# A graph network with routed experts: the second product of the first layer's experts by seven block products

## The chip, the cores and the metric

The kernel runs on one core of one Trainium2 chip. A core has a matrix engine (TensorE, PE in the profile, with its weight loads shown as PEld), a vector engine (VectorE, DVE), an engine for activation functions (ScalarE, ACT), a general one (GpSimd, POOL) and one that mostly starts transfers (SyncE, SP). Each works through its own list of instructions in order, and waits for the others through semaphores. Data lie in HBM, in the core's memory of 128 partitions (SBUF), or in the banks into which TensorE sums (PSUM). The metric is the device time of one execution in microseconds (us); the figure used is the median of several runs.

## The reference

There are 3327 nodes with 256 features, and an adjacency matrix of 3327 by 3327 with few entries. Two layers follow each other:

```
x = x + relu(adj @ (layernorm(x) @ W) + b)                       # layer 0, graph
x = x + experts_0(layernorm(x))                                  # 8 experts, hidden width 1024, relu
x = x + relu(f(adj) @ (tanh(layernorm(x) @ Wp + bp) @ Wg) + bg)  # layer 1, f: tanh(adj^2), the top 700 of a row
x = x + experts_1(layernorm(x))                                  # 8 experts, hidden width 256, gelu, added to its input
```

The experts of layer 0 are what the change is about. Each token's scores for the eight experts are `x Wg^T + bg`; the two best are taken, and a softmax of the two gives their weights:

```
for e in range(8):
    h = relu(x @ W1[e].T + b1[e])
    y = h @ W2[e].T + b2[e]
    out = out + combine[:, e] * y      # combine is zero but for a token's two experts
```

The kernel computes an expert only for the tokens that chose it. All is in float32.

## The kernel before, in words

**Tokens and blocks.** The nodes are padded to 26 tiles of 128. While the graph part of layer 0 is at work, VectorE computes the routing scores of finished tiles (L659, one instruction for each tile and expert, reading the tile `gate`, which holds one layer's eight gate vectors on every partition). GpSimd then scatters each token's normalized row, with its weight and its place, into a list in HBM that is ordered by expert (`xlist`, L779). Experts work on blocks of 256 rows of that list, all of one expert. The blocks are numbered by steps `t`. There are 30 steps in the arm of the program that runs: 26 blocks of 256 rows (two row groups of 128) and four of 128 rows (one row group; "singles", at t = 12, 17, 22 and 27).

**One step.** `step` (L1231) does the following.

- It starts the loads of block `t + 2` (L1101 to L1150: the tokens' rows, the two weight matrices of 1 MB each, and the biases), on SyncE's queue, into the ring places that block `t - 1` left.
- `first` (L1164) computes the hidden layer, transposed: for each of eight pieces of 128 hidden units, two matmuls of width 256 (L1171) into one of two PSUM buffers (`psh`), and one ScalarE instruction that adds the bias and takes the relu (L1178).
- `turned` (L1152) turns the next block's tokens: four transposes on TensorE (L1157) into the same kind of buffer, and a copy to SBUF (L1161). The function that copies is a parameter of `experts`: VectorE's `tensor_copy` for layer 0, ScalarE's `copy` for layer 1.
- `second` (L1181) computes the output: for each of the two row groups, eight matmuls of width 256 that sum into one bank (L1209). VectorE adds the bias (L1216) and multiplies by the row's weight (L1217), and GpSimd scatters the 128 rows to the token's places in HBM (`ys`, L779).

**Order.** The program text is not yet the order on the engines. A planner orders each engine's instructions by its own estimates and by the data dependences. `tc.issue_after`, mostly through the helper `behind`, forces some instructions behind a named one: in the experts the indices of the scatter (L1187 to L1192) stay behind the last scaling of the block before (`last_y`), and other work for VectorE is put behind the same mark.

**Around the experts.** The first steps, t = 0 to 2, overlap the end of the graph part; the last tokens are routed during step 0, and a plan for the late blocks is made on VectorE during steps 2 and 3. During the last steps VectorE adds the outputs that are ready (`add_begun`, L1462) and computes statistics of the next normalization (L1616). After the last step, `between` (L1510) loads the other outputs from `ys` (L1280), adds them to `x` (L1293), normalizes, and computes the features for the graph part of layer 1. The gate vectors of layer 1 are loaded into the same tile `gate` by a transfer of 1 MB on GpSimd's queue (L1419), after the last score of layer 0 and step 1; the trace has its issue at 335.6 us.

Of the kernel before, what the change touches and what calls it, by code (L numbers as in the profile page):

```python
# [10 lines left out]
F32 = mybir.dt.float32  # L11
BF16 = mybir.dt.bfloat16
I32 = mybir.dt.int32
AF = mybir.ActivationFunctionType
ALU = mybir.AluOpType
# [7 lines left out]
P = 128  # L23
NT = 26
NP = NT * P
D = 256
DC = D // P
# [18 lines left out]
SG = SB // P  # L46
# [4 lines left out]
WT, ID = D, D + 1  # L51
# [61 lines left out]
def places_of(loads, ends, free):  # L113

    at = {}
    for i, q in enumerate(loads):
        at[q] = free[i] if i < RING else at[ends[i - RING]]
    return at, [at[q] for q in ends[len(loads) - RING :]]
# [3 lines left out]
AT0, BLOCKS0 = places_of(LOADS[0], ENDS[0], list(range(RING)))  # L122
# [5 lines left out]
def gnn_moe_two_layers(  # L128
# [24 lines left out]
    nc = tc.nc  # L153
# [3 lines left out]
    work = ctx.enter_context(tc.tile_pool(name="work", bufs=3))  # L157
    dram = ctx.enter_context(tc.tile_pool(name="dram", bufs=1, space=bass.MemoryType.DRAM))
    psh = ctx.enter_context(tc.tile_pool(name="psh", bufs=2, space=PSUM))
    psy = ctx.enter_context(tc.tile_pool(name="psy", bufs=4, space=PSUM))  # L160
# [24 lines left out]
    def blk(name, n):  # L185

        at = blk_places[name][blk_at[name] % len(blk_places[name])]
        blk_at[name] += 1
        return pad[:, at : at + n]

    proj_sb = const.tile([P, DC, D], F32, name="proj_sb")
    gates = []
# [74 lines left out]
    rows = slots[:, 0 : NP // SB]  # L267
# [18 lines left out]
    rows_written, early_rows, outputs, last_product, last_y = [], [], [], [], []  # L286
# [6 lines left out]
    def behind(instructions):  # L293

        if instructions and any(i is instructions[-1].ins for i in nc.cur_bb.bb.instructions):
            return tc.issue_after(instructions[-1].ins)
        return nullcontext()

    def by_feature(name, w, t=None):
        if t is None:  # L300
            t = const.tile([P, DC, w.shape[1]], F32, name=name)
        nc.gpsimd.dma_start(out=t, in_=w.rearrange("(c p) n -> p c n", p=P))
        return t
# [13 lines left out]
    gate = state.tile([P, E, D], F32, name="gate")  # L317

    def load_gate(g):
        nc.gpsimd.dma_start(  # L320
            out=gate.rearrange("p e d -> p (e d)"),
            in_=g.rearrange("e d -> (e d)").unsqueeze(0).partition_broadcast(P),
        )
# [453 lines left out]
    def scatter(a, index, rows_, group):  # L777

        d = nc.gpsimd.indirect_dma_start(  # L779
            out=a[:, :],  # L780
            out_offset=bass.IndirectOffsetOnAxis(ap=index, axis=0),
            in_=rows_,
            in_offset=None,
        )
        tc.declare_no_dep(d.ins, group=group, reason="all have rows of their own")
        tc.add_to_no_dep_group(group, d.ins)
        return d
# [258 lines left out]
        nc.vector.tensor_tensor(aside, spare_, aside, ALU.subtract)  # L1046
        return end

    def experts(xlist, ys, group, fixed, n_hidden, func, w1T, b1, w2T, b2, copy, order_of_places, kept=None):

# [4 lines left out]
        hc_n = n_hidden // P  # L1057
# [13 lines left out]
        loaded, started = [], []  # L1071
# [23 lines left out]
        def col_of(t):  # L1095
            return t if t < EARLY else order[t - EARLY]

        def groups_of(t):
            return SG if t < EARLY or order[t - EARLY] < LATE_PAIRS else 1

        def load(late):  # L1101

            with behind([b[0] for b in loaded[-1:]]):
                load_one(late)
# [56 lines left out]
            copy(xT, pt)  # L1161
            return xT

        def first(xT, w1, bb1, n):  # L1164

            hT = blk("narrow" if kept else "wide", hc_n * SB)
            hT = hT.rearrange("p (c b) -> p c b", b=SB)[:, :, 0 : n * P]
            for hc in range(hc_n):
                ps = psh.tile([P, n * P], F32, name="ps_h", tag="ph")
                for c in range(DC):  # L1170
                    nc.tensor.matmul(  # L1171
                        ps,
                        lhsT=w1[:, c, ts(hc, P)],
                        rhs=xT[:, c, :],
                        start=(c == 0),
                        stop=(c == DC - 1),
                    )
                nc.scalar.activation(hT[:, hc, :], ps, func, bias=bb1[:, hc : hc + 1])  # L1178
            return hT

        def second(t, late, hT):  # L1181
            _, xb, _, _, w2, bb2 = loaded[t]
            col, n = col_of(t), groups_of(t)
            index = work.tile([P, SG], I32, name="index", bufs=6)[:, 0:n]
            with behind(last_y):
                if t < EARLY:
                    nc.vector.tensor_copy(index, xb[:, :, ID])  # L1187
                else:
                    _, own, aside = late[0:3]
                    index_f = index.bitcast(F32)  # L1190
                    nc.vector.tensor_tensor(index_f, xb[:, :, ID], own[:, col, 0:n], ALU.mult)
                    nc.vector.tensor_tensor(index, index_f, aside[:, col, 0:n], ALU.add)  # L1192
            if t >= own_n:
                e = expert(t, late, [PE, DVE])
                w2 = all_w2[:, ds(e, 1), :, :].rearrange("p o c d -> p (o c) d")
                bb2 = all_b2[:, ds(e, 1), :].rearrange("p o d -> p (o d)")
            if not kept:
                y = blk("narrow", SG * D).rearrange("p (g d) -> p g d", d=D)
            else:
                if not several:  # L1200
                    wide = blk("wide", H // P * SB)
                    for at in range(0, H // P * SB, SG * D):
                        y = wide[:, at : at + SG * D]
                        several.append(y.rearrange("p (g d) -> p g d", d=D))
                y = several.pop(0)
            for g in range(n):
                ps = psy.tile([P, D], F32, name="ps_y", tag="py")
                for hc in range(hc_n):
                    last_product[:] = [nc.tensor.matmul(  # L1209
                        ps,  # L1210
                        lhsT=hT[:, hc, ts(g, P)],
                        rhs=w2[:, hc, :],
                        start=(hc == 0),
                        stop=(hc == hc_n - 1),
                    )]
                nc.vector.tensor_tensor(y[:, g, :], ps, bb2, ALU.add)  # L1216
                last_y[:] = [nc.vector.tensor_scalar(  # L1217
                    y[:, g, :], y[:, g, :], xb[:, g, WT : WT + 1], None, ALU.mult
                )]
                d = scatter(ys, index[:, g : g + 1], y[:, g, :], "outputs" + group)  # L1220
                tc.declare_no_dep(d.ins, group="read" + group, reason="not rows read by then")
                outputs.append(d)

        ready = {}

# [5 lines left out]
        def step(late, end=always, place=None, between=None):  # L1231

            t = len(started)
            started.append(t)
            while len(loaded) < min(t + RING // places, end):
                load(late)
            if t not in ready:
                ready[t] = turned(loaded[t][1], groups_of(t))
            _, _, w1, bb1, _, _ = loaded[t]
            hT = first(ready.pop(t), w1, bb1, groups_of(t))  # L1240
            if between:
                between()
            if t + 1 < min(len(loaded), end):
                ready[t + 1] = turned(loaded[t + 1][1], groups_of(t + 1), place)
            second(t, late, hT)

        def steps_to(late, stop):
            while len(started) < stop:
# [116 lines left out]
    def count(pan, k, copied):  # L1365
# [7 lines left out]

    layer0 = experts(
        xlist0, ys0, "0", FIXED[0], H, AF.Relu, f0_w1T, f0_b1, f0_w2T, f0_b2,
        nc.vector.tensor_copy, BLOCKS0,
    )

    def tiles_of(pans):
# [35 lines left out]
    with tc.issue_after(last_product[0].ins):  # L1415
        list_waiting()


    load_gate(gates[1])  # L1419
    by_feature(None, g1_wp, proj_sb)  # L1420
    nc.gpsimd.dma_start(out=gnn_b_sb, in_=g1_bg[0:1, :].partition_broadcast(P))
    ng = NPAN * PW // GROUP
# [2 lines left out]
        pc, lhsT=ones, rhs=positive.rearrange("p n i k -> p (n i k)"), start=True, stop=True  # L1425
    )
    sums = const.tile([1, ng], F32, name="most_sums")
# [8 lines left out]
    late = plan(positive.rearrange("p n i k -> p (n i k)"))  # L1436
# [33 lines left out]
    second = []  # L1470
# [38 lines left out]

    def between():  # L1510

        normal.clear()
        second.clear()
        waiting = []
        for pair in turned_pairs():
            waiting.append(pair)
            if len(waiting) > 1:
                second_features(*waiting.pop(0))
        second_features(*waiting.pop(0))
        outputs.clear()  # L1520
        rows_written.clear()

        piece_at.clear()
        piece_at.update(AT1)
        expect(LOADS[1])
        for pan in range(ahead):
            n_loads = len(begun) + (NCHUNK if pan == 0 else 0)
            load_pieces(NCHUNK, filter_behind, output_loads[0:n_loads])
# [77 lines left out]
    with tc.If(first_usual > 0) as arms:  # L1606
# [28 lines left out]
        with tc.If(second_usual > 0) as inner:  # L1635
            layer1.know(2 * E)
            waiting, asked, added, k = [], [], [], 0
            while len(layer1.started) < layer1.always:
# [8 lines left out]
                with behind(last_y):  # L1647
                    if asked and asked[0][2] + 1 < at <= layer1.always - FIXED[1]:
                        yt, tiles, _ = asked.pop(0)
                        add_loaded(yt, *tiles)  # L1650
                        added.append(tiles)
                if waiting and at > waiting[0][1] + (1 if k < FIRST_TILES // 2 else 2):
                    tiles, _, written = waiting.pop(0)
# [190 lines left out]
```

## Time and profile before

| | us |
|---|---|
| median of 3 runs | 1220.21 (1218.53 to 1228.95) |
| the profiled execution | 1222.4 |
| its span in the profile | 1220.7 |
| PE busy in the span | 1176.8 |
| DVE busy | 755.1 |
| ACT busy | 524.4 |
| POOL busy | 288.2 |
| mean granted clock of TensorE | 0.982 |

The profile is of one execution, and durations below are from it; the span is the time from its first to its last instruction. A line of the groups reads: source line, engine, operation, output and inputs by the names of their tiles, shape, number of instructions, then the busy time and the mean of one in ns, and the idle time of the engine ahead of them with what ended it. A line of a timeline has the start, the length, and then the same, with several equal instructions in a row drawn together. A float32 matmul shows as two records, so 16 of them are "x32". "Granted clock" is the share of full speed that the chip allowed TensorE. The experts of layer 0 lie between about 285 and 720 us.

### The profile page before, as it was taken

The page shows a single profiled execution, that of the slowest core. Times are in us where ns is not written, and L with a number is a line of the kernel's source. Part 1 is how long each engine was busy: PE and PEld are TensorE (multiplying, and loading weights), DVE is VectorE, ACT ScalarE, POOL GpSimd, SP SyncE. Part 2 cuts the span into 40 slices and gives each one's busy share as a digit, 9 for nine tenths or more (in the row PEclk, how much of TensorE's full clock was granted, in tenths as well). Part 3 has the DMA queues.
Part 4 walks back from the last instruction along what each step waited for, and adds up shares of the span by engine and source line. Part 5 has one row for each costly group of instructions (what it writes and reads, how often), then busy time and mean ns, then how long its engine had stood idle before and what let it go on. Part 6 is the DMA issues. An engine that isn't in the chain of part 4 may idle for free. (4 is left out here: it accounts for less than half of the span.)

```text
span 1220.7 us, 18191 instructions
## 1 busy us (share of the span) xinstructions
PE 1176.8 (96%) x5689; PEld 1008.2 (83%) x5689; DVE 755.1 (62%) x2767; ACT 524.4 (43%) x977; POOL 288.2 (24%) x367
## 2 busy tenths in 40 slices
PE   8999999999899999999999999999999999988983
PEld 7888888888688888888888888888888888877863
DVE  7699999988761111111121359289999998784464
ACT  5689566521222222323222236985555542132331
POOL 1112233043421111111111110022242242264441
PEclk9999999999899999999999999999999999988996
DMA  9894747654376555756565946154455452556696
GB/s 344 187 317 189 246 160 202 226 178 139 99 243 209 185 191 172 263 177 219 195 213 181 366 160 230 56 186 180 143 196 186 149 185 66 175 176 213 207 294 214
DMA packets 123178, 241.59 MB, mean 198 GB/s; under 512 B 24480, under 2 KB 93120, under 8 KB 116160
## 3 DMA queue, kind: packets, MB, share of 16 engines
q1 hardware_dynamic: 108656, 205.59, 51.0%
q0 software_dynamic: 11136, 31.60, 7.0%
q10 hardware_dynamic: 3280, 3.15, 0.7%
q8 instruction: 47, 0.77, 0.3%
q14 instruction: 59, 0.48, 0.1%
HBM read 203.98 MB, written 36.33 MB: 197 GB/s over the span
## 5 line engine op out<-in xcount | busy, mean ns | idle before, releaser
L440 PE MATMUL ps_g<-s,ring 128*128 128x256 f32 x1352 | 294.2, 380 | 0.0
L440 PEld LDWEIGHTS ps_g<-s,ring 128*128 128x128 f32 x1352 | 256.3, 190 | 34.0
L1178 ACT ACTIVATE pad<-ps_h,ring 128x256 f32<-128x256 f32 (+1 forms) x282 | 128.3, 457 | 346.3 <-PE ps_h L1171 321.7
L1171 PE MATMUL ps_h<-pad,ring 128*128 128x256 f32 (+1 forms) x1184 | 259.0, 372 | 9.5 <-ACT pad L1178 6.0
L1171 PEld LDWEIGHTS ps_h<-pad,ring 128*128 128x128 f32 x1184 | 205.8, 193 | 55.0 <-ACT pad L1178 18.9
L1209 PE MATMUL ps_y<-ring,pad 128*128 128x256 f32 x928 | 209.7, 382 | 0.0
L659 DVE SCALAR_TENSOR_TENSOR rt_product<-xn,gate 128x256 f32<-128x256 f32 x400 | 195.1, 488 | 16.2 <-ACT xn L360 2.2
L779 POOL DMA_INDIRECT ys<-pad,index x114 | 112.9, 990 | 390.5 <-DVE pad L1217 259.4
L1209 PEld LDWEIGHTS ps_y<-ring,pad 128*128 128x128 f32 x928 | 173.9, 192 | 22.1 <-issue 0.2
L779 POOL DMA_INDIRECT xlist<-xn,rt_idx x104 | 114.5, 1101 | 154.4 <-DVE ln_nw L347 56.3
L1369 ACT ACTIVATE sign<-ring,below 128x416 bf16<-128x416 f32 x208 | 133.4, 642 | 11.6 <-DMA ring<-in_adjT 5.6
L470 PE MATMUL ps_g<-ring,pad 128*128 128x256 f32 x520 | 115.5, 380 | 0.7 <-DMA ring<-in_adjT 0.5
L1216 DVE TENSOR_TENSOR pad<-ps_y,ring 128x256 f32<-128x256 f32 x64 | 27.1, 423 | 136.2 <-PE ps_y L1209 127.8
L470 PEld LDWEIGHTS ps_g<-ring,pad 128*128 128x128 f32 x520 | 98.3, 190 | 14.8 <-DMA ring<-in_adjT 0.9
L1161 DVE COPY pad<-ptb 128x512 f32<-128x512 f32 (+1 forms) x29 | 18.9, 652 | 144.6 <-PE ptb L1157 143.6
L1534 ACT ACTIVATE ring<-ring 128x3328 f32<-128x3328 f32 x22 | 65.4, 2979 | 87.6 <-DVE ring L1533 50.2
L470 PE MATMUL ps_g<-ring,s 128*128 128x256 f32 x390 | 89.6, 379 | 0.1
L470 PEld LDWEIGHTS ps_g<-ring,s 128*128 128x128 f32 x390 | 74.1, 190 | 10.4 <-ACT xnT L538 0.5
L480 DVE TENSOR_TENSOR ring<-ring,ring 128x768 f32<-128x768 f32 (+1 forms) x80 | 79.8, 1013 | 0.0
L495 PE MATMUL ps_g<-ring,s 128*128 128x256 f32 x312 | 68.5, 380 | 3.0 <-ACT s L360 3.0
L495 PEld LDWEIGHTS ps_g<-ring,s 128*128 128x128 f32 x312 | 59.0, 190 | 11.6 <-ACT s L360 3.6
L1535 ACT ACTIVATE ring<-ring 128x3328 f32<-128x3328 f32 x22 | 65.4, 2977 | 0.6
(220 smaller groups left out, 1114.8 us busy)
## 6 DMA issues: line engine op xcount, KB each, us to landing
ring<-in_adjT SPq DMA_DIRECT2D x50, 1664.0 KB
ring<-in_f_w1T SPq DMA_DIRECT2D x30, 1024.0 KB
ring<-in_f_w2T SPq DMA_DIRECT2D x30, 1024.0 KB
ring<-xlist SPq DMA_DIRECT2D x52, 258.0 KB
ring<-in_f_w SPq DMA_DIRECT2D x36, 256.0 KB
ring<-ys SPq DMA_DIRECT2D x12, 512.0 KB
ring<-in_f_b SPq DMA_DIRECT2D x34, 128.0 KB
xlist<-h2T SPq DMA_DIRECT2D x16, 257.0 KB
```

What stands on the lines that cost most here:

```text
L440: nc.tensor.matmul(ps[it], lhsT=chunks[k][:, c, ts(it, P)], rhs=s[:, j, :], start=(j == 0), stop=(j == NT - 1),)
L470: nc.tensor.matmul(ps, lhsT=b[:, c, :], rhs=a[:, c, :], start=(first and c == 0), stop=(c == CJ - 1), skip_group_check=not first,)
L480: nc.vector.tensor_tensor(out[:, part, :], out[:, part, :], other[:, part, :], ALU.add)
L495: nc.tensor.matmul(sums[pan][c], lhsT=s[:, j, ts(c, P)], rhs=piece(pan, j // CJ)[:, j % CJ, :], start=(j == 0), stop=(j == NT - 1),)
L659: nc.vector.scalar_tensor_tensor(product, xn, 1.0, gate[:, e, :], ALU.mult, ALU.mult, accum_out=sc[:, g, e : e + 1],)
L779: d = nc.gpsimd.indirect_dma_start(out=a[:, :], out_offset=bass.IndirectOffsetOnAxis(ap=index, axis=0), in_=rows_, in_offset=None,)
L1171: nc.tensor.matmul(ps, lhsT=w1[:, c, ts(hc, P)], rhs=xT[:, c, :], start=(c == 0), stop=(c == DC - 1),)
L1178: nc.scalar.activation(hT[:, hc, :], ps, func, bias=bb1[:, hc : hc + 1])
L1209: last_product[:] = [nc.tensor.matmul(ps, lhsT=hT[:, hc, ts(g, P)], rhs=w2[:, hc, :], start=(hc == 0), stop=(hc == hc_n - 1),)]
L1369: nc.scalar.activation(sign, piece(pan, k)[:, :, ts(i, GROUP)], AF.Sign, bias=below, accum_out=positive[:, pan, i, k : k + 1],)
L1534: nc.scalar.activation(a, a, AF.Square)
L1535: nc.scalar.activation(a, a, AF.Tanh)
```

## The change

For steps from t = 3 on whose block has two row groups (23 of the 30), the second product is computed by `second_seven`. The hidden layer `h` is cut into two row groups and two halves of the hidden units, and the weights into two halves of the hidden units and two halves of the output columns. Where eight products of these blocks gave the output (two for each of its four parts), seven products of sums of blocks do:

```
t1 = B12 - B11      t2 = B22 - t1      t3 = B22 - B12      t4 = B21 - t2
s1 = A21 + A22      s2 = s1 - A11      s3 = A11 - A21      s4 = A12 - s2
C11: A11 B11 + A12 B21
C12: (A11 B11 + s2 t2) + (s1 t1 + s4 B22)
C21: (A11 B11 + s2 t2 + s3 t3) + A22 t4
C22: (A11 B11 + s2 t2 + s3 t3) + s1 t1
```

Here `A` are the four blocks of `h` (row group, half of the hidden units) and `B` those of the weights (half of the hidden units, half of the columns). A product is four matmuls with 128 columns, summed in a bank; some go on in a bank that was read before, as the brackets show.

- `prepare` makes the four sums of the weights on VectorE, in the tile `gate`, which is free by then, and has ScalarE write bias times weight into the output rows (two instructions). It stands ahead of `first` in the program text.
- `difference` makes `s3` as soon as half of the hidden layer is there; `s1`, `s2`, `s4` follow `first`.
- `put_in` takes a bank times the row's weight and adds it to a part of the output: seven VectorE instructions of 128 by 128 take the place of the two pairs L1216 and L1217.
- The four banks of `psy` are all used in each step.
- The turned tokens of layer 0 are copied by ScalarE in all 30 steps.
- The gate vectors of layer 1 are loaded at the start of `between`, since the sums lie in their tile until then.

```diff
+        def prepare(t):
+            _, xb, _, _, w2, bb2 = loaded[t]
+            flat = gate.rearrange("p e d -> p (e d)")
...
+            nc.vector.tensor_tensor(t1, halves(w2, 0, 1), halves(w2, 0, 0), ALU.subtract)
+            nc.vector.tensor_tensor(t2, b22, t1, ALU.subtract)
+            nc.vector.tensor_tensor(t4, b21, t2, ALU.subtract)
+            nc.vector.tensor_tensor(t3, b22, halves(w2, 0, 1), ALU.subtract)
+            y = blk("narrow", SG * D).rearrange("p (g d) -> p g d", d=D)
+            for g in range(SG):
+                nc.scalar.activation(y[:, g, :], bb2, AF.Copy, scale=xb[:, g, WT : WT + 1])
...
+        def difference(sums, hT):
+            a11, a21 = halves(hT, 0, 0), halves(hT, 0, 1)
+            nc.vector.tensor_tensor(sums[1][2], a11, a21, ALU.subtract)
...
                 nc.scalar.activation(hT[:, hc, :], ps, func, bias=bb1[:, hc : hc + 1])
+                if sums and hc == hc_n // 2 - 1:
+                    difference(sums, hT)
...
+        def second_seven(t, late, hT, sums):
+            (t1, t3, t2, t4), (s1, s2, s3, s4), y = sums
...
+            nc.vector.tensor_tensor(s1, a21, a22, ALU.add)
+            nc.vector.tensor_tensor(s2, s1, a11, ALU.subtract)
+            nc.vector.tensor_tensor(s4, a12, s2, ALU.subtract)
+            ps_x, ps_q, ps_b, ps_z = (
+                psy.tile([P, P], F32, name="ps_y", tag="py") for _ in range(4)
+            )
+            def multiply(ps, a, b, first=True):
+                for c in range(hc_n // 2):
+                    last_product[:] = [nc.tensor.matmul(
+                        ps, lhsT=a[:, c, :], rhs=b[:, c, :], start=(first and c == 0),
+                        stop=(c == hc_n // 2 - 1), skip_group_check=not first,
+                    )]
+            def put_in(g, half_, ps):
+                part = y[:, g, ts(half_, P)]
+                last_y[:] = [nc.vector.scalar_tensor_tensor(
+                    part, ps, xb[:, g, WT : WT + 1], part, ALU.mult, ALU.add
+                )]
+            multiply(ps_x, a11, b11)
+            put_in(0, 0, ps_x)
+            multiply(ps_q, a22, t4)
+            put_in(1, 0, ps_q)
+            multiply(ps_b, a12, b21)
+            put_in(0, 0, ps_b)
+            multiply(ps_z, s1, t1)
+            put_in(1, 1, ps_z)
+            multiply(ps_x, s2, t2, False)
+            put_in(0, 1, ps_x)
+            multiply(ps_z, s4, b22, False)
+            put_in(0, 1, ps_z)
+            put(y, index, 0)
+            multiply(ps_x, s3, t3, False)
+            put_in(1, 0, ps_x)
+            put_in(1, 1, ps_x)
+            put(y, index, 1)
...
+            sums = prepare(t) if seven and t >= seven and groups_of(t) == SG else None
+            hT = first(ready.pop(t), w1, bb1, groups_of(t), sums)
...
     layer0 = experts(
         xlist0, ys0, "0", FIXED[0], H, AF.Relu, f0_w1T, f0_b1, f0_w2T, f0_b2,
-        nc.vector.tensor_copy, BLOCKS0,
+        nc.scalar.copy, BLOCKS0, seven=3,
     )
...
-    load_gate(gates[1])
     by_feature(None, g1_wp, proj_sb)
...
     def between():
+        load_gate(gates[1])
         normal.clear()
```

More of the change, by code (lines that the diff above doesn't have):

```diff
@@ L1047, in places, with experts @@
         return end
-    def experts(xlist, ys, group, fixed, n_hidden, func, w1T, b1, w2T, b2, copy, order_of_places, kept=None):
+    def experts(xlist, ys, group, fixed, n_hidden, func, w1T, b1, w2T, b2, copy, order_of_places, kept=None,
+                seven=None):
         own_n, all_w2, all_b2, all_b1 = kept or (EARLY + LATE, None, None, None)
@@ L1162, in turned, with halves, first @@
             return xT
-        def first(xT, w1, bb1, n):
+        def halves(a, k, i):
+            return a[:, k * hc_n // 2 : (k + 1) * hc_n // 2, ts(i, P)]
+        def prepare(t):
+            _, xb, _, _, w2, bb2 = loaded[t]
+            flat = gate.rearrange("p e d -> p (e d)")
+            n = hc_n // 2 * P
+            sums = [flat[:, i * n : (i + 1) * n].rearrange("p (c d) -> p c d", d=P) for i in range(4)]
+            t1, t3, t2, t4 = sums
+            b21, b22 = halves(w2, 1, 0), halves(w2, 1, 1)
+            nc.vector.tensor_tensor(t1, halves(w2, 0, 1), halves(w2, 0, 0), ALU.subtract)
[5 more added lines that the diff above has]
+                nc.scalar.activation(y[:, g, :], bb2, AF.Copy, scale=xb[:, g, WT : WT + 1])
+            tokens_ = [
+                work.tile([P, DC, 2 * P], F32, name=name, bufs=2).rearrange(
+                    "p c (h d) -> p (c h) d", d=P
+                )
+                for name in ("xnT", "xnT", "h2T", "h2T")
+            ]
+            return sums, tokens_, y
+        def difference(sums, hT):
+            a11, a21 = halves(hT, 0, 0), halves(hT, 0, 1)
+            nc.vector.tensor_tensor(sums[1][2], a11, a21, ALU.subtract)
+        def first(xT, w1, bb1, n, sums=None):
             hT = blk("narrow" if kept else "wide", hc_n * SB)
@@ L1178, in first, with place_of @@
                 nc.scalar.activation(hT[:, hc, :], ps, func, bias=bb1[:, hc : hc + 1])
-            return hT
-        def second(t, late, hT):
-            _, xb, _, _, w2, bb2 = loaded[t]
-            col, n = col_of(t), groups_of(t)
+                if sums and hc == hc_n // 2 - 1:
+                    difference(sums, hT)
+            return hT
+        def place_of(t, late):
+            xb, col, n = loaded[t][1], col_of(t), groups_of(t)
             index = work.tile([P, SG], I32, name="index", bufs=6)[:, 0:n]
@@ L1192, in second, with put @@
                     nc.vector.tensor_tensor(index, index_f, aside[:, col, 0:n], ALU.add)
+            return index
+        def put(y, index, g):
+            d = scatter(ys, index[:, g : g + 1], y[:, g, :], "outputs" + group)
+            tc.declare_no_dep(d.ins, group="read" + group, reason="not rows read by then")
+            outputs.append(d)
+        def second_seven(t, late, hT, sums):
+            (t1, t3, t2, t4), (s1, s2, s3, s4), y = sums
+            _, xb, _, _, w2, _ = loaded[t]
+            index = place_of(t, late)
+            a11, a12, a21, a22 = (halves(hT, k, i) for i in range(2) for k in range(2))
+            b11, b21, b22 = halves(w2, 0, 0), halves(w2, 1, 0), halves(w2, 1, 1)
+            nc.vector.tensor_tensor(s1, a21, a22, ALU.add)
[3 more added lines that the diff above has]
+                psy.tile([P, P], F32, name="ps_y", tag="py") for _ in range(4)
+            )
+            def multiply(ps, a, b, first=True):
[26 more added lines that the diff above has]
+            put(y, index, 1)
+        def second(t, late, hT):
+            _, xb, _, _, w2, bb2 = loaded[t]
+            n = groups_of(t)
+            index = place_of(t, late)
             if t >= own_n:
@@ L1219, in second @@
                 )]
-                d = scatter(ys, index[:, g : g + 1], y[:, g, :], "outputs" + group)
-                tc.declare_no_dep(d.ins, group="read" + group, reason="not rows read by then")
-                outputs.append(d)
+                put(y, index, g)
         ready = {}
@@ L1239, in step @@
             _, _, w1, bb1, _, _ = loaded[t]
-            hT = first(ready.pop(t), w1, bb1, groups_of(t))
+            sums = prepare(t) if seven and t >= seven and groups_of(t) == SG else None
+            hT = first(ready.pop(t), w1, bb1, groups_of(t), sums)
             if between:
@@ L1244, in step @@
                 ready[t + 1] = turned(loaded[t + 1][1], groups_of(t + 1), place)
-            second(t, late, hT)
+            if sums:
+                second_seven(t, late, hT, sums)
+            else:
+                second(t, late, hT)
         def steps_to(late, stop):
```

## The prediction

> **What bounds the kernel now.** I read the page first: busy shares, then the slices.
>
> ```profile
> PE 1176.8 (96%) x5689; PEld 1008.2 (83%) x5689; DVE 755.1 (62%) x2767; ACT 524.4 (43%) x977; POOL 288.2 (24%) x367
> ...
> DVE  7699999988761111111121359289999998784464
> ...
> PEclk9999999999899999999999999999999999988996
> ...
> L1209 PE MATMUL ps_y<-ring,pad 128*128 128x256 f32 x928 | 209.7, 382 | 0.0
> L1216 DVE TENSOR_TENSOR pad<-ps_y,ring 128x256 f32<-128x256 f32 x64 | 27.1, 423 | 136.2 <-PE ps_y L1209 127.8
> ```
>
> TensorE is busy 96% of the span, and VectorE waits for its products (127.8 us at L1216), not the reverse; VectorE's 62% is an average of stages at 90% and a stage at 10% (slices 13 to 23, the first layer's experts). So I cut the span by stage, for the experts:
>
> ```profile
> core 0: us, PE busy (x) PEld busy (x) DVE busy (x) ACT busy (x) POOL busy (x), PEclk, DMA share, GB/s
> ...
> 500.00:600.00 100.00, 99.92 (x490) 84.24 (x489) 17.52 (x50) 27.01 (x59) 12.57 (x13) 1.00 0.63 206
> ```
>
> PE has no idle time there; VectorE has 82% free. The same stage as a timeline of PE, one block (start, length):
>
> ```profile
> 645.91 0.60 PE L1157 MATMUL ptb<-ident,ring 128*128 128x128 f32 x4
> 646.34 7.07 PE L1209 MATMUL ps_y<-ring,pad 128*128 128x256 f32 x32
> 653.25 7.16 PE L1171 MATMUL ps_h<-pad,ring 128*128 128x256 f32 x32
> 660.24 0.60 PE L1157 MATMUL ptb<-ident,ring 128*128 128x128 f32 x4
> ```
>
> From start to start: transposes 0.43 us, second product 6.91, first product 6.99; 14.33 a block. An f32 matmul leaves two records, so 16 matmuls are x32 and one record costs 6.91 / 32 = 0.216. A block costs what PE issues. The rest of the chip matters only if it makes PE wait.
>
> [...] the trace shows the granted clock at a half in stretches of 3.4 or 6.8 us (310.6 to 317.4, 1082.0 to 1088.8 and others) after PE gaps of 1.3 to 4.0 us. [...]
>
> **A. Seven products for eight (gain).** Only blocks with t from 3 and two row groups: 30 steps less t = 0, 1, 2 and four singles, 23 blocks. Each issues 7 x 4 = 28 matmuls of width 128, 56 records, for 16 of width 256. The width-128 f32 products of before are those of a single; on PE's timeline:
>
> ```profile
> 489.19 1.05 PE L1171 MATMUL ps_h<-pad,ring 128*128 128x128 f32 x8
> 490.08 0.60 PE L1209 MATMUL ps_y<-ring,pad 128*128 128x256 f32 x2
> ```
>
> 8 records in 490.08 - 489.19 = 0.89: 0.1115 each. 56 x 0.1115 = 6.24, against 6.91: 0.67 saved a block, 23 x 0.67 = 15.4 us. This is the thin point: 28 x 128 columns for 16 x 256 is an eighth less, 0.86, and 0.19 of that goes to the shorter products. Longer runs in the singles (12 and 16 records, with waits for ScalarE in them) give 0.117: 6.55, saving 8.3 in all. [...]
>
> **B. Turned copies on ScalarE, gate later, around block 0 (285 to 345).** Here VectorE is 75% busy with the scores, and PE has its largest gap of this stage (PE, then VectorE):
>
> ```profile
> 311.63 3.78 PE L1171 MATMUL ps_h<-pad,ring 128*128 128x256 f32 x8 [4.01 <-ACT pad L1178]
> ...
> 294.12 0.69 DVE L1161 COPY pad<-ptb 128x512 f32<-128x512 f32 x1 [1.02 <-remote]
> ```
>
> PE waits for relus; ScalarE stood behind a routing step that waits for VectorE's chain (L724 to L725, 4.61 us idle). The copy at 294.12 lies in that chain with its wait: 0.69 to 1.7 us leave it, so the gap shrinks by 0.6 to 1.6. The half clock after it could shorten too, at most 1.7 more. I take -1.5 (-0.6 to -3.3). The copy itself is 585 ns on ScalarE by the second layer's rows; in later steps it sits while PE runs the 6.2 us second product: nothing. Moving the 1 MB gate load from 335.6 frees the queues while block 3's operands come; they had landed in time (about 340, needed 341): nothing gained.
>
> **C. Two prefills a block on ScalarE (loss).** They are written ahead of the first product, and land between relus, which come every 0.88 us while PE has only two buffers for them:
>
> ```profile
> 655.24 0.47 ACT L1178 ACTIVATE pad<-ps_h,ring 128x256 f32<-128x256 f32 x1 [0.40 <-PE ps_h L1171]
> ```
>
> The gap is 0.40. No row shows a copy of 128x256 from SBUF with a weight. The rows of L1546 (832 elements, 907 ns) and L1534 (3328, 2979) give 0.83 ns an element; from 642 ns at 416 (L1369) this is 642 - 160 x 0.83 = 509, which I take as 0.51 (0.43 to 0.59); neighbours on ScalarE overlap by 0.11 (two L388 copies of 0.588 in 1.08), leaving a step of 0.40, which just fits. In the issue order one lies behind relu 1 and one behind relu 2. Only in the four blocks after a single do both fall into one gap: 2 x 0.40 - 0.40 less what a second buffer hides, about 0.3 each, 1.2. I take +1.5; 0 if all is hidden, +5 if each of the 46 costs 0.1.
>
> **D, E. VectorE's added work (loss).** [...] L1293's row of that size has 689; follow-on instructions step 0.61 (five of 128x1024, 1219 each, take 5.76). Per block 4 sums of w2, one difference and 3 sums of hT: 8 x 0.61 = 4.9. Seven put-ins of 128x128 from PSUM (no row; L1216 at 256 columns has 423, [...] L907 has 278 from SBUF, and steps are some 40 shorter than records): 7 x 0.25 = 1.8, for 2 x (423 + 363) = 1.6 before. With the index 6.9 us of a block's 13.7: half, so it can't be the bound by amount, only by order. VectorE runs in order: s1, s2, put-in 1, s4, put-ins 2, 3, 4, t1 of the next block, 5, t2, 6, t4, the two of 7, t3. Where PE waits: product 4 needs s1, done 1.5 us after the first product, and starts 3 x 0.89 = 2.7 after it; product 6 goes on in the bank that put-in 4 reads, which ends about 0.2 + 0.3 after product 4, while product 5 gives 0.89; product 7 needs put-in 5, which follows t1: ends about 1.45 after product 4, needed at 1.78. Slack 0.2 to 0.4 each. I take +0.5 (0 to +5, 0.2 a block). In the last two steps VectorE also has the additions of ready outputs (5.8 and 1.2 us at t = 28) and statistics (4.7 at t = 29) ahead of s1: +0.5 (0 to +3).
>
> **F. Gate load in the gap between the layers.** It is a POOL-queue DMA of 1 MB that must wait for the last put-in (it overwrites the sums), and falls between the last two scatters in POOL's order. The loads of ys wait for these scatters, and VectorE for the loads:
>
> ```profile
> 727.53 2.48 DVE L1293 TENSOR_TENSOR x<-x,ring 128x1024 f32<-128x1024 f32 x2 [3.50 <-DMA ring<-ys]
> ```
>
> At the 400 GB/s moved there, 1 MB is 2.5 us; the last scatter would be 1 to 2.5 late. PE at this point has other work for about 3 us before it needs the normalized rows (busy 52.3 of 717 to 770). So +0.5; 0 to +3. Its reader, the second layer's scores, comes at about 797.
>
> **Sum.** -15.4 - 1.5 + 1.5 + 0.5 + 0.5 + 0.5 = -13.9. The profiled execution took 1222.4 (span 1220.7), 2.2 over the median of the runs: 1222.4 - 13.9 = 1208.5, and for a median 1220.2 - 13.9 = **1206.3**. The second layer is unchanged, but its half-clock windows near the end (four) can fall otherwise when all is shifted: 3 us either way.
>
> **Rivals.**
> - *More gain, about 1201*: [...] 0.14.
> - *Partial, about 1214*: the cadence is 0.117 as in the longer runs (8.3), or prefills delay relus by 0.1 each. For it: the fit in 0.40 is exact to hundredths, and those longer runs are the nearer length. 0.22.
> - *Slower, about 1240*: the chain put-in 4, t1, put-in 5 comes late for product 7, in each block. Its break-even is 0.67 us a block, against a slack of 0.3: put-ins and sums would have to take 1.0 more than here. If a stall reaches the 1.3 us after which the clock was halved, a window of 3.4 us costs 1.7: (1.3 + 1.7 - 0.67 - 0.1) x 23 is some +50, half of the blocks some +20. Against: the 689 and 423 rows would have to be off by half. 0.15.
> - *It does not do what it says* (the products not seven in each full block): no, 23 blocks have 28 matmuls in PE's order.
>
> **Numbers.** Forecast (1203 to 1210) 0.49, more 0.14, partial 0.22, slower 0.15. About 1% (12.2 us) is what a measurement of this kernel can tell: the bound is 1208.0. Faster: most of the forecast's case (0.36) and the gain case, 0.50; within: 0.35; slower 0.15. The range 1199 to 1222 leaves out the slower case and the edge of the gain case.
>
> **What would show it.** A: x56 of 128x128 at L1209's place in 6.2 to 6.3 us and a block of 13.7. B: the gap at 307 near 3. C: relus still every 0.88, idle before them 0. E: no PE idle before products 6 and 7. F: additions (L1293) at most 2 us later against the end of block 29. Wrong if the cadence of 56 records is over 0.12, or if PE waits for put-ins in the steady block.

## The result, and the profile after

The changed kernel takes 1335.53 us (median of 4 runs, 1332.67 to 1341.61), the kernel before 1221.73 in the same comparison (4 runs): the ratio is 1.0916, with a 95% interval of 1.0882 to 1.0949. It is 9% slower, where 1.1% faster was forecast. The profiled execution took 1341.6, its span 1339.9.

Page of the changed kernel, the lines that answer to those of before, and one that is new:

```profile
PE 1209.8 (90%) x6241; PEld 1043.0 (78%) x6241; DVE 868.6 (65%) x3013; ACT 556.4 (42%) x1053; POOL 291.1 (22%) x367
...
PE   8999999998887878778797899999999999998983
...
PEclk9999999998987888889889898999999999999996
...
L1203 PE MATMUL ps_h<-pad,ring 128*128 128x256 f32 (+1 forms) x1184 | 305.4, 414 | 82.4 <-ACT pad L1210 79.2
...
L1182 ACT ACTIVATE pad<-ring,ring 128x256 f32<-128x256 f32 x46 | 23.2, 506 | 107.8 <-DMA ys<-pad,index 88.6
```

The row of the first product before, and 100 us of the experts' stage in the changed kernel (a row of the windows: PE's busy time first; 0.86 is the granted clock):

```profile
L1171 PE MATMUL ps_h<-pad,ring 128*128 128x256 f32 (+1 forms) x1184 | 259.0, 372 | 9.5 <-ACT pad L1178 6.0
```

```profile
545.00:645.00 100.00, 81.15 (x451) 69.83 (x451) 32.43 (x80) 26.75 (x61) 9.70 (x10) 0.86 0.46 152
```

TensorE is no longer full in the experts' stage (the 11th to the 24th digit of its slices), and its clock is lower there: 0.86 in this stretch, 1.00 before. The span grew by 119.2. Two terms of one row make up that much: the first product (L1203, L1171 before) has 82.4 us of idle time ahead of it where it had 9.5, and takes 305.4 us where it took 259.0, with as many matmuls. That is 72.9 of waiting, nearly all of it for ScalarE, and 46.4 of slower products. The rest cancels: TensorE's other work is 13.4 us shorter (its busy time grew by 33.0 in all), and its other idle time 13.3 longer. The last line of the page says what ScalarE waits for. L1182 writes bias times weight into the output rows, 46 times; ahead of it ScalarE is idle 107.8 us, 88.6 of that until a scatter into `ys` has landed.

One block of the changed kernel from its stall on, on PE's timeline (start, length, what, idle time before and what ended it):

```profile
600.28 6.53 PE L1203 MATMUL ps_h<-pad,ring 128*128 128x256 f32 x16 [4.40 <-ACT pad L1210]
606.65 0.60 PE L1158 MATMUL ptb<-ident,ring 128*128 128x128 f32 x4
607.09 1.06 PE L1249 MATMUL ps_y<-ring,pad 128*128 128x128 f32 x8
607.98 1.06 PE L1249 MATMUL ps_y<-gate,pad 128*128 128x128 f32 x8
608.88 1.06 PE L1249 MATMUL ps_y<-ring,pad 128*128 128x128 f32 x8
609.77 1.95 PE L1249 MATMUL ps_y<-gate,xnT 128*128 128x128 f32 x16
611.55 1.06 PE L1249 MATMUL ps_y<-ring,h2T 128*128 128x128 f32 x8
612.45 1.06 PE L1249 MATMUL ps_y<-gate,h2T 128*128 128x128 f32 x8
613.34 7.16 PE L1203 MATMUL ps_h<-pad,ring 128*128 128x256 f32 x32
```

The seven products take 613.34 - 607.09 = 6.25 us, as forecast, and PE waits for nothing between them. All the loss is ahead of them: PE stands still for 4.40 us in the middle of the first product, and the second half of it (16 records) then takes 606.65 - 600.28 = 6.37 us instead of 3.5 (half of the 6.99 before); the mean granted clock in it is 0.55. ScalarE in the same block:

```profile
594.22 0.47 ACT L1210 ACTIVATE pad<-ps_h,ring 128x256 f32<-128x256 f32 x1 [0.40 <-PE ps_h L1203]
599.36 0.51 ACT L1182 ACTIVATE pad<-ring,ring 128x256 f32<-128x256 f32 x1 [4.67 <-DMA ys<-pad,index]
599.77 0.46 ACT L1210 ACTIVATE pad<-ps_h,ring 128x256 f32<-128x256 f32 x1
600.71 0.51 ACT L1182 ACTIVATE pad<-ring,ring 128x256 f32<-128x256 f32 x1 [0.48 <-DMA ys<-pad,index]
```

And GpSimd's scatters, which are the ones waited for:

```profile
592.64 0.97 POOL L779 DMA_INDIRECT ys<-pad,index  x1 [18.11 <-issue]
593.91 0.97 POOL L779 DMA_INDIRECT ys<-pad,index  x1 [0.30 <-DVE index L1225]
```

So the chain is: the block just ended scatters its rows at 592.6 and 593.9; the scatters land about 5.8 us after GpSimd has done with each (3.2 and 4.8 in the block before); the instruction that writes bias times weight stands between the second and third relu and waits for the landing; the relus behind it wait on ScalarE; PE fills its two PSUM buffers and stops. In ScalarE's instruction list these instructions read the weight and the bias of ring places 0 and 3, while the relus around them read their bias from ring place 4: they belong to the *next* block. The trace agrees: the first two (343.48 and 346.55) fall into the first product of block 2, which has none of its own, and the last block has none between its relus (824.66 to 830.80). The planner has taken them one block ahead. The output rows have two places in turn, so the next block's place is the one that the scatter just issued still reads.

### The profile page after: what moved, and what is told of

Same layout as the page of the kernel before. It is cut to its first block, busy times and chain, and to the rows that moved or that the text cites. A ratio compares the mean times of both kernels' runs of the same rounds, so it can differ in the third digit from the quotient of the medians.

```text
span 1339.9 us, 19711 instructions
## 1 busy us (share of the span) xinstructions
PE 1209.8 (90%) x6241; PEld 1043.0 (78%) x6241; DVE 868.6 (65%) x3013; ACT 556.4 (42%) x1053; POOL 291.1 (22%) x367
## 3 DMA queue, kind: packets, MB, share of 16 engines
q10 hardware_dynamic: 3280, 3.15, 0.7%
## 5 line engine op out<-in xcount | busy, mean ns | idle before, releaser
L1203 PE MATMUL ps_h<-pad,ring 128*128 128x256 f32 (+1 forms) x1184 | 305.4, 414 | 82.4 <-ACT pad L1210 79.2
L1203 PEld LDWEIGHTS ps_h<-pad,ring 128*128 128x128 f32 x1184 | 234.5, 217 | 141.4 <-ACT pad L1210 98.1
L1210 ACT ACTIVATE pad<-ps_h,ring 128x256 f32<-128x256 f32 (+1 forms) x282 | 125.5, 454 | 325.8 <-PE ps_h L1203 250.9
L1194 DVE TENSOR_TENSOR h2T<-pad 128x512 f32<-128x512 f32 x23 | 15.9, 691 | 128.8 <-ACT pad L1210 128.8
L1240 DVE TENSOR_TENSOR xnT<-pad 128x512 f32<-128x512 f32 x23 | 15.9, 692 | 94.5 <-ACT pad L1210 94.5
L1256 DVE SCALAR_TENSOR_TENSOR pad<-ps_y,ring,pad 128x128 f32<-128x128 f32 x184 | 62.0, 348 | 15.4 <-PE ps_y L1249 15.2
L1182 ACT ACTIVATE pad<-ring,ring 128x256 f32<-128x256 f32 x46 | 23.2, 506 | 107.8 <-DMA ys<-pad,index 88.6
```

The costliest lines, as they stand in the source:

```text
L1203: nc.tensor.matmul(ps, lhsT=w1[:, c, ts(hc, P)], rhs=xT[:, c, :], start=(c == 0), stop=(c == DC - 1),)
L1256: last_y[:] = [nc.vector.scalar_tensor_tensor(part, ps, xb[:, g, WT : WT + 1], part, ALU.mult, ALU.add)]
```

## The experiments

Ratios are to the kernel before, run beside each version on the same chip; its median was 1208 us in these comparisons (1221.73 in the first).

**Behind the own block's relus.** The two instructions leave `prepare` (first lines), and are issued in `second_seven` (last lines) behind the last relu of their own block:

```diff
-            for g in range(SG):
-                nc.scalar.activation(y[:, g, :], bb2, AF.Copy, scale=xb[:, g, WT : WT + 1])
...
+            with behind(last_relu):
+                for g in range(SG):
+                    nc.scalar.activation(y[:, g, :], bb2, AF.Copy, scale=xb[:, g, WT : WT + 1])
```

> The changed kernel with one edit: the two ScalarE instructions that write bias times weight are issued behind the last relu of their own block, instead of between the relus of the block before. Theory (they wait there for the scatters of the block before that one, and hold up the relus, and after them TensorE): nothing to wait for is left, and the block takes the predicted 13.7 us; 1200 to 1215. Rival (VectorE's longer chain or the seven products are what costs): stays at 1300 or more.

Measured: 1201.68, ratio 0.9946 (0.9926 to 0.9965). Moving two instructions a block takes away the whole loss. ScalarE's timeline, and the block on PE's (its start to the start of the next first product):

```profile
560.43 0.47 ACT L1208 ACTIVATE pad<-ps_h,ring 128x256 f32<-128x256 f32 x1 [0.41 <-PE ps_h L1201]
560.81 0.49 ACT L1238 ACTIVATE pad<-ring,ring 128x256 f32<-128x256 f32 x1
561.21 0.57 ACT L1162 COPY pad<-ptb 128x512 f32<-128x512 f32 x1
561.67 0.52 ACT L1238 ACTIVATE pad<-ring,ring 128x256 f32<-128x256 f32 x1
```

```profile
553.18 7.16 PE L1201 MATMUL ps_h<-pad,ring 128*128 128x256 f32 x32
...
566.86 7.16 PE L1201 MATMUL ps_h<-pad,ring 128*128 128x256 f32 x32
```

The instructions (L1238) wait for nothing, and a block takes 566.86 - 553.18 = 13.68 us, 0.66 less than the 14.34 of before (653.25 to 667.59). But 23 x 0.66 = 15.2, and the run gained only 0.54% of 1208.65, 6.5 us (4.2 to 8.9). Two gaps of PE that the kernel before doesn't have are taken up below.

**The products left as they were.** Only the two ScalarE instructions are added to the kernel before, ahead of the first product, and VectorE adds the eight products to the prepared rows:

```diff
+            y = prefilled(t) if not kept and t >= 3 and groups_of(t) == SG else None
             hT = first(ready.pop(t), w1, bb1, groups_of(t))
...
-                nc.vector.tensor_tensor(y[:, g, :], ps, bb2, ALU.add)
-                last_y[:] = [nc.vector.tensor_scalar(
-                    y[:, g, :], y[:, g, :], xb[:, g, WT : WT + 1], None, ALU.mult
-                )]
+                last_y[:] = [nc.vector.scalar_tensor_tensor(
+                    y[:, g, :], ps, xb[:, g, WT : WT + 1], y[:, g, :], ALU.mult, ALU.add
+                )]
```

> The kernel before, with eight products as they were, and only the bias times weight written by ScalarE ahead of the first product and one VectorE instruction of 128x256 that adds the products to it, for the same 23 blocks. Theory: the wait for the scatters comes with these instructions, and the 117 + 14 us that the change lost against the forecast show up here: about 1340, 1300 to 1370. Rival (the loss needs the seven products or VectorE's sums): 1215 to 1230.

Measured: 1328.37, ratio 1.0977 (1.0916 to 1.1037). The list of waits of this run (us in total, times, the longest) has the same line, and a larger sum (the changed kernel has 88.6 us in 34 waits):

```profile
ACT pad L1186 <- DMA ys<-pad,index: 186.9, 36, 10.2
```

The loss comes without the seven products and without VectorE's sums.

**A third place for the output rows.** The instructions are pinned behind the second and third relu of the block before their own, about where the planner had put them, and the output rows take three places in turn:

```diff
+                if after and hc in (1, 2):
+                    prefill(after, hc - 1, relu)
...
+            at = (blk_places["narrow"] + blk_places["xT_arms"])[len(turns) % 3]
+            turns.append(at)
```

> The changed kernel with the same two instructions at the same place in ScalarE's order, behind the second and third relu of the block before, but with three places for the output rows in turn instead of two, so that they wait for scatters that are one block older. Theory: the wait goes though the order stays; 1200 to 1220, the upper part if the position between relus costs some tenths a block. Rival (two more instructions between relus are too much for ScalarE, wait or no wait): above 1280.

Measured: 1231.55, ratio 1.0188 (1.0143 to 1.0234), above the range of the theory and far below the rival. The trace has eight waits for scatters left, 16.8 us in all, where the changed kernel has 34. They come in pairs: one near the start, three in the second full block behind one of a single row group. A full block takes its place while the block before it is still at its first product, a block of one row group (and those with t under 3) only at its second; where the two kinds meet, the turns are out of step, and the third place is again the one just scattered. So a further run fixes each step's place by its number:

```diff
-            at = (blk_places["narrow"] + blk_places["xT_arms"])[len(turns) % 3]
-            turns.append(at)
+            at = (blk_places["narrow"] + blk_places["xT_arms"])[t % 3]
```

> As the run with three places for the output rows, but each step's place is its number modulo three, so that no instruction waits for the scatter of the block just ended, also around the blocks of one row group, where the run with three places in order of their taking still did. Position on ScalarE as there. Theory: of the 29 us between that run and the one with the instructions behind their own relus, the waits for scatters (four pairs of about 1.7 + 2.1 us with the half clock after them) go; what stays is waits for the next block's bias after the blocks of one row group, some 3 us in all, and the position between relus: 1200 to 1212 where that job's kernel before has 1208. Rival (the position itself costs): 1220 or more.

Measured: 1206.35, ratio 0.9994 (0.9973 to 1.0016). No wait for a scatter is left. ScalarE's timeline in a full block:

```profile
582.34 0.47 ACT L1219 ACTIVATE pad<-ps_h,ring 128x256 f32<-128x256 f32 x1 [0.40 <-PE ps_h L1212]
582.71 0.50 ACT L1177 ACTIVATE pad<-ring,ring 128x256 f32<-128x256 f32 x1
583.22 0.47 ACT L1219 ACTIVATE pad<-ps_h,ring 128x256 f32<-128x256 f32 x1
583.59 0.50 ACT L1177 ACTIVATE pad<-ring,ring 128x256 f32<-128x256 f32 x1
584.09 0.47 ACT L1219 ACTIVATE pad<-ps_h,ring 128x256 f32<-128x256 f32 x1
```

Each fits into the gap of 0.40, and the block takes 13.68 us as with the other position. The same position, without the wait, costs a full block nothing. The run is 0.5% (some 6 us) above the one behind the own relus. Its trace has waits of ScalarE for the next block's bias, whose load has not landed so early after the short blocks: 7.2 us in four, the longest 4.7. That these are the whole difference was not tried.

**The small parts alone.** The turned copies by ScalarE (`nc.scalar.copy` in the call of `experts`), and the gate load moved into `between`, each as the only edit to the kernel before:

> The kernel before with only the turned tokens of the first layer copied by ScalarE. As forecast (part B): 1.5 us less (0.6 to 3.3), that is a ratio of 0.997 to 1.0, the gap of TensorE near 307 us down from 4.0 to about 2.5. Rival (the copies delay relus or the moves shift the order for the worse): 2 to 6 us more.

> The kernel before with only the second gate's load moved to the start of the part between the layers. As forecast (part F): 0 to 3 us more, ratio 1.000 to 1.0025, with the additions of the outputs up to 2 us later. Rival (the load was in the way of block 3's operands): 1 to 3 us less.

Measured: the copies 1.0019 (1.0007 to 1.0032), the gate load 1.0002 (0.9983 to 1.0022). With the copies PE's gap of block 0 is 2.65, and still the time is 2.3 us longer, not 1.5 shorter: in the rival's range. Of the gap, too, only a part is due to the copies: the profile of the kernel before (4.01) is from another comparison, and the run of the gate load, on the same chip as the copies, has 3.15. Where the 2 to 4 us went stays open. In its profiled execution the version with the copies has TensorE busy for 275.43 of the first 285 us, ahead of any expert, where the one with the gate load has 278.41; in five other profiles it lies between 275.87 and 278.68, and one profile of each can't tell whether the copies set it.

The run of the gate load tests less than its name says. The planner issued that load at 667.6 us, among the last blocks, where no sums hold the tile; in the changed kernel it stands between the last two scatters (838.26). So 1.0002 says that moving it away from 335.6 gains nothing; it doesn't price the load in the gap between the layers.

**The two gaps.** The run behind the own relus has these gaps on PE (first fence), and this on VectorE at that time (second):

```profile
343.25 0.17 PE L792 MATMUL pc<-cum,ones_sq 128*128 128x8 bf16 x1 [4.70 <-DVE rt_row L764]
...
690.52 2.09 PE L1250 MATMUL ps_y<-gate,xnT 128*128 128x128 f32 x16 [2.38 <-DVE xnT L1241]
```

```profile
339.69 0.69 DVE L1176 TENSOR_TENSOR gate<-ring 128x512 f32<-128x512 f32 x1 [6.25 <-DMA ring<-in_f_w2T]
...
682.30 5.76 DVE L1385 TENSOR_TENSOR x<-x,s 128x1024 f32<-128x1024 f32 x5
```

The first (in the changed kernel the same wait of VectorE is 1.85, and PE has no gap there): VectorE reaches the first sum of block 3's weights at 333.4, and waits 6.25 us for their load. The last routing step (L764) is queued behind it, PE's count (L792) waits for that, and block 2's first product is queued behind the count on PE. The second: the additions of ready outputs (5.76 us, then 1.22) stand ahead of step 28's `s1` (L1241), which comes too late for the fourth product. The edits:

```diff
-        nc.scalar.copy, BLOCKS0, seven=3,
+        nc.scalar.copy, BLOCKS0, seven=4,
```

```diff
         layer0.step(late)
-        layer0.step(late)
         with behind(last_y):
             add_begun()
         layer0.step(late)
+        layer0.step(late)
```

> As the run with the two ScalarE instructions behind their own block's relus, and the seven products only from t = 4 on. Theory: TensorE's new gap of 4.7 us at 338.5, where VectorE waits for block 3's weights before it can serve the routing, is gone, for 0.7 us given up: 3 to 5 us less than with t = 3, ratio to before 0.990 to 0.992. Rival (the wait only moves to block 4's weights): ratio as with t = 3, 0.994 to 0.996.

> The run before this one, with the additions of the ready outputs put behind step 26 instead of step 27, where VectorE is idle for 8 us. Theory: the stall of 2.6 us ahead of the fourth product of step 28 goes: ratio to before 0.987 to 0.990. Rival (the outputs have not landed by then, or the stall moves to step 27): no gain over the run before this one, or a loss of up to 3 us.

Measured: 0.9908 (0.9881 to 0.9936), as the theory has it, then 0.9861 (0.9832 to 0.9890), 1191.64 us, a little below its range. In the last run both gaps are gone; VectorE does the 5.76 us of additions at 664.9, in time in which it was idle. It is the fastest version with the products by seven, 1.4% under the kernel before.

**Copies back on VectorE in that version** (`nc.vector.tensor_copy` again):

> As the run with the products from t = 4 on and the earlier additions, with the turned tokens copied by VectorE as before the change. From the run of the copies alone (0.2% slower): 2 us less, ratio to before 0.983 to 0.986. Rival (0.69 us more in VectorE's chain ahead of the fourth and fifth product now delay TensorE, or block 0's gap grows back): up to 4 us more, ratio 0.986 to 0.990.

Measured: 0.9872 (0.9836 to 0.9909), 1192.16. That lies in the rival's range, but the interval holds the 0.9861 of the version with ScalarE's copies as well: no gain of 2 us shows, and no loss that could be told.

## Why the prediction was wrong

**The step that failed is C.** It said that the two prefills "land between relus" and that in the issue order "one lies behind relu 1 and one behind relu 2", and priced their duration. It priced them as instructions of the block whose relus they stand between. They are the next block's, and so need an output place that the block just ended is still scattering. The forecast named no wait for C at all. In the kernel before the same rule holds for VectorE's L1216, but a whole block later, when the scatter has landed; taken one block ahead it became a wait of 88.6 us on the engine that empties TensorE's two buffers. C was put at +1.5, at most +5. The run with the eight products and these instructions alone has it at +9.8% of 1208.65, 118 us (111 to 125). What C did price was right: 0.51 us a piece was estimated and 0.506 measured, the step is the 0.40 that was taken (though by the lines read for it, 2 x 0.588 - 1.08, neighbours overlap by 0.10, not 0.11), and two of them fit between relus without cost.

**A was right.** 6.24 us forecast for 56 records of width 128, 6.25 measured; 0.67 saved a block, 0.66 measured. The 0.117 of the longer runs had waits in it; 56 records in a row (0.1116 us each) are no slower than eight (0.1115). Of the 23 blocks, the best version keeps 22.

**B had the gap's direction right and the sum wrong.** PE's gap near 307 is 2.65 with the copies alone and was 4.01 before, but on one chip it is 2.65 against 3.15: 0.5, under the 0.6 to 1.6 that were forecast. The total rose by 0.19% instead of falling. "Nothing gained" for the gate load stands (1.0002). But the statement that block 3's operands were in time held only for the first product. The weights of the second product are now needed at its sums, and there VectorE, which runs in order, waited 6.25 us for them in the run behind the own relus: 4.70 on PE, a term that the sum lacked.

**D was too small.** +0.5 was taken for the additions ahead of `s1`, and 2.38 + 0.22 of idle time on PE came in the run behind the own relus, 3.49 in the one from t = 4. The run with the additions elsewhere is 0.5% faster, some 6 us, though the two intervals overlap.

**E was right, and F in its price.** In the steady block PE never waits for put-ins, sums or differences, though a put-in takes 348 ns where L907's row of that size, from SBUF, has 278; its step, 0.26, was taken as 0.25. The sums and differences of 128x512 take 691 and 692 ns (L1194, L1240), where L1293's row of 128x512 before has 689. In F the gate load stands between the last two scatters, as forecast. From the end of GpSimd's last scatter to the loads of `ys` it is 3.70 us in the changed kernel (840.14 to 843.84) and 1.65 before (720.38 to 722.03): the scatter is 2 us late, within the 1 to 2.5. The additions come 12.4 us after the last product, 9.6 before, so 2.8 later, where the prediction's sign was at most 2. PE had no gap there (busy 52.4 of the 53 us from 838 on, 52.3 before), so little can have been lost; no run tries it alone.

**The rivals.** The slower one had the wrong mechanism: the stall is not in VectorE's chain. Its second half did come about. Half clock followed the stalls of TensorE, and the first product is 46.4 us longer with it. Where 4.40 us of idle time went ahead, the next 16 records had a mean clock of 0.55 (600.28 to 606.65) and took 1.8 times as long. Gaps of only 1.83 and 1.78 us (up to 577.36 and 580.26) were followed by a mean clock of 0.50 for 5.3 us (to 585.54), so in this trace shorter gaps, one soon after the other, went with half clock too. The 1.3 us that this rival reckoned with did not always bring it: in the kernel before, the clock was 0.50 from 279.9 to 283.3, behind a gap of 1.32, but 1.00 from 329.45 to 334, behind one of 1.98. The rival of more gain, about 1201, was the author's estimate, and no run shows it: the 56 records take 0.1116 us each, as forecast.

With the wait removed and the two gaps closed, the forecast of -13.9 us is met by -16.8 (-13.3 to -20.3). The sum of the other terms was of the right size, though not each of them: that version has 22 blocks and the additions elsewhere, and B alone measured 2.3 us the other way.

## What to carry to other kernels

When a planner orders the work, an instruction written "ahead" can be issued a whole iteration ahead; look up by its operands whose iteration it belongs to, and ask for each buffer that it writes who last reads it and when that read has ended, a transfer's landing included. Where such a wait sits on an in-order engine, price it by what is queued behind it (here relus, and behind them two PSUM buffers of TensorE: with 88.6 us of waiting on ScalarE came 72.9 of idle time and 46.4 of slower products), and not by the instruction's own length. A sum or copy that uses an operand earlier than before moves the deadline of that operand's load as well (here VectorE waited 6.25 us for the weights of block 3).

## What the runs showed of the hardware

- Runs of 56 records of float32 products of width 128 keep the cadence of 0.1116 us (6.25 / 56), with weight loads whose records last 192 ns.
- A scatter of 128 rows of 256 floats landed about 5.8 us after GpSimd's instruction ended (593.61 to 599.36, 594.88 to 600.71), while SyncE's loads of a coming block, issued from 591.9 on, were under way; in the block before it was 3.2 and 4.8. That these loads are what made it slow was not tried.
- With gaps of TensorE of 1.8 to 4.4 us in block after block, the mean granted clock from 545 to 645 us is 0.86 in the changed kernel, with 81.15 of 100 us busy. If the clock was either full or half, that is half speed in about 28 of the 100 us, an estimate from the mean: (1 - 0.86) / 0.5.
- The kernel before has a median of 1221.73 in the first comparison and 1208 in three later ones, which is as large a difference as the whole gain that the change could bring; only ratios within one comparison tell it.
